# The tail of a fused attention and Fourier kernel: weight rows loaded earlier, the spectrum scaled in 8 and 24 rows, and the transform back along h in two halves

## The chip, the cores and the metric

The kernel runs on one core of a Trainium2 chip. The metric is the time of one execution on the device in microseconds; the median of several executions is compared. Engines are named as in the profile: PE (TensorE; PEld is its weight load), DVE (VectorE), ACT (ScalarE), POOL (GpSimd), SP (SyncE, which here only issues DMAs).

## The reference, cut to what matters

Two layers act on x (4, 64, 96, 96), both as x + f(group_norm(x)). The first is an attention over all 9216 positions of an image (with a sigmoid in place of the softmax), followed by a gate per channel. The second multiplies the lowest 32 by 16 Fourier modes by complex weights, 64 input by 64 output channels for each mode:

```python
u_hat = jnp.fft.rfft2(u, norm='ortho')
top = jnp.einsum('bchw,cohw->bohw', u_hat[:, :, :k_h, :k_w], R_pos)
bot = jnp.einsum('bchw,cohw->bohw', u_hat[:, :, H - k_h:, :k_w], R_neg)
v_hat = jnp.zeros((B, C_out, H, W_half), dtype=u_hat.dtype)
v_hat = v_hat.at[:, :, :k_h, :k_w].set(top)
v_hat = v_hat.at[:, :, H - k_h:, :k_w].set(bot)
return jnp.fft.irfft2(v_hat, s=(H, W), norm='ortho')
```

Everything is float32.

## The kernel before, in words

The four images are handled as two pairs; 128 partitions hold two images' 64 channels. The attention of both pairs is one long stream on PE and ACT (lines 580, 601, 618). The second layer of the first pair is hidden inside the stream of the second. The second layer of the second pair can only begin when the stream has ended: this is the tail, and the change lies there. An image pair is cut into 12 strips of 768 columns (`NSTRIP`, `STRIP`).

The steps of the tail, in order of time:

- Reload of the layer's input. `again` lies in the space of `vT`; the last piece is issued by SP at L880 when the stream ends. Seven strips are combined with it on DVE (L183), five (`ADDED`: 4, 5, 6, 8, 10) are scaled on ACT (L983) and completed by an accumulating DMA that POOL issues (L984).
- Strips. For each, DVE transposes (L991, into `xt`, places `t0` to `t3`), ACT sums squares (L996), and PE transforms along w (L1003). After each third of the strips DVE transposes the result (L1009, places `a0` to `a2`) and PE transforms along h (L1015).
- Spectrum. DVE transposes (L1050, place `s`), then DVE and ACT scale by the group's deviation into `u` (L1055 to L1063), in two halves of 16 of the 32 rows `h`; between them the constant mode is corrected (L215).
- Mixing. For each `q` from 0 to 7 four rows `h` are multiplied by their weight rows (L230), in two halves that are copied out by DVE and by ACT in turn (L125, L127). The results of `q` 0 to 5 go through DRAM (`vd`, issued by SP at L248) and come back in another order as `vt` (L286, issued by ACT and SP); those of `q` 6 and 7 are put in place by a matrix `picks` on PE (L269) and added by DVE (L274).
- Transform back along h. 16 matmuls (L1105), each with 64 rows of input, two of which sit side by side in the array, one for each image; then eight transposes on DVE (L1112).
- Transform back along w: for each strip four matmuls (L1122, two halves of the strip, two halves of the rows), one addition on DVE to the strip of x1 (L1130; strip 0 in two halves) and one output DMA (L1131, SP and ACT in turn). `ps_y` has three buffers.

The 32 weight rows of the mixing arrive from several sides: nine in `early` during the stream, two and four (`w_mid`) in the tail's own space, nine by POOL into the space of `vT` as the strips are done with it (L1072), and the last eight by SP (L941) into the places `a0`, `t0` to `t3`, `a1`, `a2` and `s`, each as soon as its place is free. SP issues its DMAs in the order of the program.

`occupy(n, ...)` sends n matmuls without use to PE behind a given instruction (L964): four before the strips, three after the statistics, one after the `picks`, three after the transform back along h.

The scheduling: inside `with tc.manual_schedule(...)` each engine runs its instructions in the order in which they are written; elsewhere in the tail a list scheduler orders them.

Of the kernel before, what the change touches and what calls it, by code (L numbers as in the profile page):

```python
# [33 lines left out]
F32 = mybir.dt.float32  # L34
F32R = mybir.dt.float32r
AF = mybir.ActivationFunctionType
ALU = mybir.AluOpType
# [3 lines left out]
P = 128  # L41
B, C, H, W = 4, 64, 96, 96
# [4 lines left out]
KW = 16  # L47
KH = 32
NB = 512
# [9 lines left out]
ENGINES = {mybir.EngineType.PE, mybir.EngineType.Activation, mybir.EngineType.DVE}  # L59
LAG = 8  # L60
SIDE = 4
U = KH * KW * 4
UPAD = 4 * SIDE
STRIP = 8 * W
SQ = 32
NSQ = H // SQ
NSTRIP = N // STRIP
# [14 lines left out]
NSLOT = 6  # L82
NLATE = 3 * NSQ * P
NPICK = 2
PICK = P + 4 * (NPICK - 1)
# [3 lines left out]
def tile_kernel(ctx: ExitStack, tc: tile.TileContext, x, cst, late, spec, out):  # L89
    nc = tc.nc  # L90
    xf = x.rearrange("b c h w -> (b c) (h w)")
    outf = out.rearrange("b c h w -> (b c) (h w)")
# [6 lines left out]
    cs = const.tile([P, NCONST], F32, tag="cs", name="cs")  # L99
    xs = []  # L100
    for p in range(NPAIR):
        xt = xpool.tile([P, N], F32, tag=f"x{p}", name=f"x{p}")
        for s in range(9):
            parts = 2 if p == 0 and s == 8 else 1
            for i in range(parts):
                cols = bass.ts(parts * s + i, N // 9 // parts)
# [8 lines left out]
    def named(name, rows=P):  # L115
        return cs[:rows, PLACE[name]]

    pav, nhalf, low_sb, ident = named("pav"), named("nhalf"), named("low"), named("ident")
    turn, moved = [0], [None, None]
# [310 lines left out]
    with tc.tile_pool(name="work", bufs=1) as work, \  # L430
# [6 lines left out]
        banks = ps_s.tile([P, 8, NB], F32, tag="banks", name="banks")  # L437
        spare = [0]

        at = attp.tile([P, 14, NB], F32, tag="at", name="at")  # L440
# [10 lines left out]
        projected = [None]  # L451
# [225 lines left out]
        each, norm0, _ = stats_of(0)  # L677
        with tc.manual_schedule(engines=ENGINES):
# [17 lines left out]
            q, split_queries = first_queries()  # L696
# [25 lines left out]
        early = []  # L722
# [82 lines left out]
        while len(done) < len(sizes):  # L805

            t, was = len(done), done[-1] if done else 0
            n = max(1, -(-was // TILES))
# [76 lines left out]
        with tc.manual_schedule(engines=ENGINES):  # L885
# [5 lines left out]
            for t in range(T):  # L891
# [14 lines left out]
                i, put_by = 0, []  # L906
# [13 lines left out]
        gate, steps, f = after(1)  # L920
# [7 lines left out]
    with tc.tile_pool(name="tail", bufs=1, reuse_waits="tile") as tail, \  # L928
            ExitStack() as banks:

        def psum(name, bufs=1):
            return banks.enter_context(
                tc.tile_pool(name=name, bufs=bufs, space=PSUM, reuse_waits="tile"))
# [18 lines left out]
            wts[NSLOT - 4 + i] = w_mid[:, bass.ts(i, KW * C)]  # L952
            nc.gpsimd.dma_start(wts[NSLOT - 4 + i], spec[NSLOT - 4 + i])

        picks = tail.tile([P, SIDE * PICK], F32, tag="pick", name="picks")
        nc.gpsimd.dma_start(picks, late[:, NLATE:])

        def occupy(n, behind, pool):


            pd = pool.tile([P, NB], F32, tag="idle", bufs=1, name=f"idle_{behind.ins.name}")
            with tc.issue_after(behind.ins):
                for _ in range(n):
                    nc.tensor.matmul(pd, cs[:, :P], cs[:, :NB], start=True, stop=True)  # L964

        small_bank = psum("ps_m")
        l1 = Layer1(1, gate, lambda name: small_bank.tile([P, NB], F32, tag="m", name=name),
                    evacuate, (nc.sync, nc.scalar))
        l1.wts = wts
        occupy(4, projected[0], small_bank)  # L970
        x1 = xs[1]

        mr, steps, mv = group_stats(None, l1.bank, "l1_1")
# [54 lines left out]
        with tc.manual_schedule(engines=ENGINES):  # L1028
            for s in range(NSTRIP):
                if s not in ADDED:  # L1030
                    l1.combine(s, again[:, bass.ts(s, STRIP)])
                strip(s)
                if s in (1, 3):
                    steps[s // 2]()
                if s == 5:
                    rows_turned(0)
                    rows(0)
                if s == 9:
                    rows_turned(1)
            var = small.tile([P, 1], F32, tag="var", name="var")  # L1040
            nc.vector.tensor_reduce(var, squares, AX.X, ALU.add)
            nc.vector.tensor_scalar(mv[:, 1:2], var, 1.0 / N, None, ALU.mult)
            steps[2]()
            steps[3]()
            rows_turned(2)
            rows(1)
            rows(2)
            l1.spread(mr)
            for b in range(2):
                nc.vector.transpose(t[:, bass.ts(b, NB)],  # L1050
                                    pu[b].rearrange("q (c k) -> q k c", k=KW))
            for half in range(2):
                h = bass.ts(half, KH // 2)
                for b in range(2):
                    nc.scalar.activation(u[:, :, :, h, 0, b], tb[b][:, :, :, h], AF.Copy,  # L1055
                                         scale=l1.rs[:, 0, b:b + 1])
                    nc.vector.tensor_scalar(u[lo, :, :, h, 1, b], tb[b][hi, :, :, h],
                                            l1.rs[hi, 1, b:b + 1], None, ALU.mult)
                    if b == 0:
                        nc.vector.tensor_scalar(u[hi, :, :, h, 1, b], tb[b][lo, :, :, h],  # L1060
                                                l1.rs[lo, 0, b:b + 1], None, ALU.mult)
                    else:
                        nc.scalar.activation(u[hi, :, :, h, 1, b], tb[b][lo, :, :, h], AF.Copy,  # L1063
                                             scale=l1.rs[lo, 0, b:b + 1])
                if half == 0:
                    l1.constant_mode()
        occupy(3, l1.last, small_bank)

        for i in range(9):
            h = NSLOT + 9 + i  # L1070
            wts[h] = again[:, bass.ts(i, KW * C)]
            nc.gpsimd.dma_start(wts[h], spec[h])  # L1072
        late_rows = iter(range(NSLOT + 18, KH))
        for tag in ("a0", "t0", "t1", "t2", "t3", "a1", "a2", "s"):
            weight(tag, next(late_rows), nc.sync)

        l1.vms = [tail.tile([P, KW * C], F32, tag="vm", bufs=4, name=f"vm_{q}")
                  for q in range(4)] + early[:4]
        banks.close()
        mix_bank = psum("ps_v", 1)  # L1080
        l1.bank = lambda name: mix_bank.tile([P, NB], F32, tag="v", name=name, bufs=7)
        l1.place_of_vt = lambda: place_of("w0", "vt")
        gh = tail.tile([P, 2 * P], F32, tag="gh", name="gh_in_fours")
        for q in range(KH // 4):
            l1.mix(q, 0)
            if q == 0:
                with tc.issue_after(moved[0].ins):
                    nc.vector.memset(gh, 0.0)
                    for e in range(2):
                        nc.vector.tensor_copy(  # L1090
                            gh[:, bass.ts(e, P)].rearrange("q (j i) -> q j i", j=4)[:, :, :H // 4],
                            named("gh")[:, bass.ts(e, H)].rearrange("q (i j) -> q j i", j=4))
            l1.mix(q, 1)
        l1.pick(picks)
        occupy(1, l1.last, mix_bank)


        banks.close()
        pz_bank, NO = psum("ps_z"), C // 4
        pz = [[pz_bank.tile([P, NB], F32, tag=f"z{b}{i}", name=f"pz_{b}_{i}") for i in range(4)]  # L1100
              for b in range(2)]
        for i in range(4):
            for e in range(2):
                for b in range(2):
                    last = nc.tensor.matmul(  # L1105
                        pz[b][i][:, bass.ts(e, KW * NO)], gh[bass.ts(b, 2 * KH), bass.ts(e, P)],
                        l1.vt[bass.ts(b, 2 * KH), :].rearrange("q (k o) -> q k o", o=C)[
                            :, :, bass.ts(i, NO)], start=True, stop=True)
        z = tail.tile([P, P, SQ], F32, tag="z", name="z_1")
        for i in range(4):  # L1110
            for b in range(2):
                nc.vector.transpose(z[:, b * C + i * NO:b * C + (i + 1) * NO, :],  # L1112
                                    pz[b][i].rearrange("q (k o) -> q o k", o=NO))
        banks.close()
        py_bank = psum("ps_y", 3)
        occupy(3, last, py_bank)
        for s in range(NSTRIP):
            py = py_bank.tile([P, 2, NB], F32, tag="y", name=f"py_{s}")
            for i in range(2):
                for r in range(2):  # L1120
                    rows = bass.ts(r, C)
                    nc.tensor.matmul(py[:, r, bass.ts(i, 2 * W)], z[rows, :, 2 * s + i],  # L1122
                                     named("gw")[rows, bass.ts(r, 2 * W)], start=True, stop=True)
            for i in range(2 if s == 0 else 1):
                n = STRIP // 2 if s == 0 else STRIP
                cols = slice(s * STRIP + i * n, s * STRIP + i * n + n)
                o = x1[:, cols].rearrange("q (i r m) -> q i r m", r=2, m=2 * W)
                from_py = py[:, :, 2 * W * i:2 * W * i + n // 2].rearrange(
                    "q r (i m) -> q i r m", m=2 * W)
                nc.vector.tensor_tensor(o, from_py, o, ALU.add)  # L1130
                (nc.sync, nc.scalar)[(s + i) % 2].dma_start(outf[bass.ts(1, P), cols], x1[:, cols])  # L1131


def _constants(l0):
# [24 lines left out]
    for b in range(2):  # L1159
        rows = slice(b * C, (b + 1) * C)  # L1160
        at = PLACE["wv"].start
        for i, w in enumerate(("wv", "wq", "wk")):
            n = len(l0[w])
# [29 lines left out]
    for n in range(SIDE):  # L1193
        pick = np.zeros((P, PICK))
        for g in range(4):
            for slot in range(2):
                for i in range(2):
                    pick[32 * g + 4 * n + 2 * slot + i, 64 * i + 32 * slot + KH - 4 + g] = 1.0
        b.append(pick)
    return a, np.concatenate(b, 1).astype(np.float32)  # L1200


# [28 lines left out]
```

## Time and profile before

| | us |
|---|---|
| median of 4 runs | 3028.34 (3027.92 to 3029.68) |
| the profiled execution, its own time | 3031.53 |
| its span in the profile | 3029.7 |
| end of the attention stream (last L618) | 2950.0 |
| first matmul of the mixing (L230) | 2982.9 |
| first matmul of the transform back along h (L1105) | 3003.4 |
| first addition of a strip (L1130) | 3012.9 |
| end of the last addition | 3023.6 |

Times inside the profile are counted from the start of the span. In the rows of the chain of waits the columns are start, length and what ran. In rows by group they are line, engine, operation, output<-inputs, shape and count, then busy time, mean duration in ns, and the idle time of the engine ahead of them. In rows by stretch they are the stretch, its length, the busy time of PE, PEld, DVE, ACT and POOL with the number of instructions, the TensorE clock that was granted as a share of the full one, the mean busy share of the 16 DMA engines, and GB/s. A float32 matmul shows as two records.

### The profile page before, as it was taken

The numbers are of one execution on the slowest core, as the hardware profiler recorded it, in microseconds if no ns is written. First come the engines' busy times: TensorE is split into PE (matmuls) and PEld (weight loads), VectorE is DVE, ScalarE is ACT, GpSimd is POOL, SyncE is SP. The second block draws the span as 40 slices with busy tenths as digits, with TensorE's granted clock in tenths as the row PEclk, the third lists the DMA queues.
The fourth block names the chain that finished last, engine by engine and source line by source line (L and its number), as shares of the span: only waits on it lengthen the run. The fifth ranks groups of instructions, "written<-read, shape, count | busy, mean of one in ns | idle before, by whom it ended". The sixth has DMA issues, their size and how long they took to land.

```text
span 3029.7 us, 44108 instructions
## 1 busy us (share of the span) xinstructions
PE 3011.0 (99%) x19364; PEld 1113.2 (37%) x19364; DVE 308.2 (10%) x706; ACT 2416.8 (80%) x1555; POOL 69.9 (2%) x138
## 2 busy tenths in 40 slices
PE   9999999999999999999999999999999999999998
PEld 4333333333333333333433333333333333333336
DVE  6300000000000000002411101100000000000006
ACT  4788888888888888887788887778778888888873
POOL 0100000000000000001300000000001000000001
PEclk9999999999999999999999999999999999999999
DMA  4100000000000000001422322412113000000027
GB/s 159 32 4 4 4 4 4 4 4 4 2 3 4 4 4 4 4 4 32 99 67 69 85 79 86 134 33 45 51 46 125 4 4 4 4 4 4 1 63 249
DMA packets 114609, 117.09 MB, mean 39 GB/s; under 512 B 77488, under 2 KB 84784, under 8 KB 114320
## 3 DMA queue, kind: packets, MB, share of 16 engines
q1 hardware_dynamic: 105536, 92.82, 11.2%
q0 software_dynamic: 7472, 18.56, 2.0%
q8 instruction: 152, 2.49, 0.3%
q10 hardware_dynamic: 1408, 2.88, 0.3%
q14 instruction: 41, 0.34, 0.0%
HBM read 79.94 MB, written 32.31 MB: 37 GB/s over the span
## 4 chain that ended last, share of the span: by engine, by line
PE 98%; DVE 1%; DMA 0%; ACT 0%; issue 0%; POOL 0%; ACTq 0%; DVEq 0%
PE banks L618 77%; PE banks L580 17%; PE banks L499 1%; PE banks L230 1%; PE banks L671 0%; DVE x L1130 0%; PE pv L230 0%; PE banks L421 0%; PE pa L1003 0%; ACT at L601 0%; PE banks L344 0%; PE pz L1105 0%; PE pu L1015 0%; PE banks L464 0%; DVE xt L991 0%
## 5 line engine op out<-in xcount | busy, mean ns | idle before, releaser
L601 ACT ACTIVATE at<-banks 128x2048 f32<-128x2048 f32 (+1 forms) x1501 | 2388.3, 1642 | 533.7 <-PE banks L580 521.8
L618 PE MATMUL banks<-at,vT 128*64 128x512 f32 (+1 forms) x11824 | 2402.2, 547 | 0.0
L618 PEld LDWEIGHTS banks<-at,vT 128*64 128x64 f32 x11824 | 778.1, 136 | 1362.3 <-issue 1307.2
L580 PE MATMUL banks<-q,kT 32*128 32x512 f32 x5040 | 542.7, 452 | 0.8 <-ACT at L601 0.7
L580 PEld LDWEIGHTS banks<-q,kT 32*128 32x128 f32 x5040 | 223.8, 182 | 447.5 <-issue 331.2
L624 DVE SCALAR_TENSOR_TENSOR x<-banks,x 128x512 f32<-128x512 f32 x36 | 24.9, 691 | 2023.1 <-PE banks L618 1945.2
L550 POOL DMA_DIRECT2D stage<-qk x96 | 47.7, 504 | 932.2 <-DMA qk<-turned 928.7
L425 DVE TENSOR_TENSOR x<-banks,x 128x768 f32<-128x768 f32 x12 | 11.5, 958 | 168.5 <-PE banks L421 168.5
L499 PEld LDWEIGHTS banks<-cs,x 64*64 64x64 f32 x1152 | 21.9, 135 | 17.3 <-ACT at L601 13.1
L506 DVE TENSOR_TENSOR vT<-banks,cs 128x256 f32<-128x256 f32 x72 | 26.8, 412 | 0.0
L499 PE MATMUL banks<-cs,x 64*64 64x80 f32 (+1 forms) x1152 | 26.0, 234 | 0.0
L626 DVE TENSOR_REDUCE maxs<-x 128x1 f32<-128x512 f32 x36 | 24.7, 686 | 1.3
L632 DVE BATCH_NORM_STATS2 stats<-x 128x6 f32<-128x512 f32 x36 | 22.5, 682 | 3.9 <-DMA x<-in_x_dram 3.9
L736 DVE COPY ws<-banks 128x512 f32<-128x512 f32 x16 | 11.1, 691 | 115.3 <-PE banks L230 115.3
L163 POOL TENSOR_TENSOR mr_l<-ve_l,cs 128x1 f32<-128x1 f32 x4 | 2.2, 558 | 837.2 <-DVE ve_l L162 837.2
L736 DVE COPY ae<-banks 128x512 f32<-128x512 f32 x6 | 4.1, 691 | 157.3 <-issue 114.9
L984 POOL DMA_DIRECT2D x<-vT x5 | 4.5, 1035 | 659.9 <-ACT x L983 659.9
L671 PE MATMUL banks<-x 128*128 128x256 f32 (+1 forms) x48 | 14.5, 464 | 4.8 <-DMA x<-in_x_dram 4.8
L580 PE MATMUL banks<-q_first,kT 32*128 32x512 f32 x144 | 17.1, 459 | 1.8 <-ACT at L601 1.1
L537 DVE STREAM_TRANSPOSE turned<-t 128x384 f32<-128x384 f32 (+1 forms) x35 | 17.9, 511 | 1.2
L170 DVE TENSOR_SCALAR x<-x,mr_l 128x512 f32<-128x512 f32 x36 | 17.6, 529 | 0.7 <-POOL mr_l L163 0.7
L1003 PE MATMUL pa<-xt,lc 128*128 128x256 f32 x72 | 16.8, 385 | 0.6 <-DVE mr_l L152 0.3
(145 smaller groups left out, 429.1 us busy)
## 6 DMA issues: line engine op xcount, KB each, us to landing
ws<-in_spec_dram SPq DMA_DIRECT2D x20, 512.0 KB
q<-qk SPq DMA_DIRECT2D x280, 32.0 KB
x<-in_x_dram SPq DMA_DIRECT2D x17, 512.0 KB
out_dram<-x SPq DMA_DIRECT2D x17, 384.0 KB
room<-in_spec_dram SPq DMA_DIRECT2D x12, 512.0 KB
old<-in_x_dram SPq DMA_DIRECT2D x12, 384.0 KB
qk<-turned SPq DMA_DIRECT2D x96, 48.0 KB
x1d<-x SPq DMA_DIRECT2D x12, 384.0 KB
```

The costliest lines, as they stand in the source:

```text
L170: nc.vector.tensor_scalar(dst, src, mr[:, 0:1], mr[:, 1:2], ALU.subtract, ALU.mult)
L230: self.last = nc.tensor.matmul(pv[bass.ts(g, 32), :].rearrange("q (n k o) -> q n k o", n=SIDE, o=C)[:, :, k, :], self.ut[:, at:at + 32], s ...
L499: projected[0] = nc.tensor.matmul(pp[bass.ts(e, P // 2), b, 2 * a + h, :width], src[rows, a, h, bass.ts(e, P // 2)], named("wv")[rows, :wi ...
L506: nc.vector.tensor_tensor(vT[:, 4 * s:4 * s + 4, bass.ts(b, C)].rearrange("p (h a) m -> p a h m", h=2), pp[:, b, :, :C].rearrange("p (a h) ...
L537: nc.vector.transpose(turned[:, k:].rearrange("p k a (m h) -> p (k a) h m", h=2), t[:, k:].rearrange("p k a h m -> p (k a) h m").bitcast(F32))
L550: nc.gpsimd.dma_start(come[bass.ts(r, QK), :], split[p][s][:, r % 2, bass.ts(r // 2, NB // 2)])
L580: nc.tensor.matmul(banks[:, bank_of(i), :], kT[r:r + 32, i % TILES // 8, i // 4 % 2, :], ask[i // TILES][r:r + 32, :], start=True, stop=True)
L601: nc.scalar.activation(at[:, of:of + n, :], banks[:, bank:bank + n, :], AF.Sigmoid)
L618: attended[0] = nc.tensor.matmul(acc[half, cols], vT[:, j, half], at[:, place(2 * pair + b), cols], start=(j == 0), stop=(j == NCH - 1 and ...
L624: nc.vector.scalar_tensor_tensor(blk, acc, 1.0, blk, ALU.mult, ALU.add, accum_out=sums[p][:, m:m + 1])
L626: mark[0] = nc.vector.tensor_reduce(maxs[p][:, m:m + 1], blk, AX.X, ALU.max)
L632: each = [lambda s=s: nc.vector.bn_stats(stats[:, s, :], xs[p][:, bass.ts(s, NB)]) for s in range(NBLK)]
```

## The change

- Four of SP's eight weight rows (24 to 27) get places of their own, `r0` to `r3`, and are issued directly behind the picks' load in the program, that is behind L880 on SP; the other four (28 to 31) follow as before into `a0`, `a1`, `a2` and `s`. The four buffers `vm` move into the places `t0` to `t3`.
- The spectrum is scaled in a part of 8 rows and one of 24.
- The matrix of the transform back along h comes from the host, in the same DMA as `picks` (1040 columns, 528 before), and is no longer arranged on DVE. It is block diagonal over the two images: one matmul takes all 128 rows and yields one half of the 96 rows h for both images, with 12 of 16 places filled.
- The transform back along h is done in two halves (`along_h_back`): the first ahead of all strips; the second in four steps whose matmuls stand between those of strips 0 to 4 and whose transposes follow the additions of strips 1 to 4. Strips 0 to 5 need the first half alone. `ps_z` keeps four banks, `ps_y` has two buffers.
- The weights of L1122 are read from `z` at a step of 16 elements, 32 before.
- Matmuls without use: three before the strips (four before), one of 256 columns after the picks (512 before), none after the transform back along h (three before).

```diff
-        picks = tail.tile([P, SIDE * PICK], F32, tag="pick", name="picks")
+        picks = tail.tile([P, SIDE * PICK + 4 * P], F32, tag="pick", name="picks")
         nc.gpsimd.dma_start(picks, late[:, NLATE:])
+        gh = picks[:, SIDE * PICK:].rearrange("q (n e m) -> q n e m", n=2, e=2)
+
+        late_rows = iter(range(NSLOT + 18, KH))
+        for i in range(4):
+            weight(f"r{i}", next(late_rows), nc.sync)
...
-        occupy(4, projected[0], small_bank)
+        occupy(3, projected[0], small_bank)
...
-            for half in range(2):
-                h = bass.ts(half, KH // 2)
+            for h in (slice(0, 8), slice(8, KH)):
...
-                if half == 0:
+                if h.start == 0:
                     l1.constant_mode()
...
-        late_rows = iter(range(NSLOT + 18, KH))
-        for tag in ("a0", "t0", "t1", "t2", "t3", "a1", "a2", "s"):
+        for tag in ("a0", "a1", "a2", "s"):
             weight(tag, next(late_rows), nc.sync)
 
-        l1.vms = [tail.tile([P, KW * C], F32, tag="vm", bufs=4, name=f"vm_{q}")
-                  for q in range(4)] + early[:4]
+        l1.vms = [place_of(f"t{q}", f"vm_{q}") for q in range(4)] + early[:4]
...
-            if q == 0:
-                with tc.issue_after(moved[0].ins):
-                    nc.vector.memset(gh, 0.0)
-                    for e in range(2):
-                        nc.vector.tensor_copy(
...
-        occupy(1, l1.last, mix_bank)
+        occupy(1, l1.last, mix_bank, NB // 2)
...
+        pz_bank, py_bank, NO = psum("ps_z"), psum("ps_y", 2), C // 4
+        z = tail.tile([P, 2, 2, C, KW], F32, tag="z", name="z_1")
+
+        def along_h_back(half, i):
+
+            pz = pz_bank.tile([P, NB], F32, tag=f"z{i}", name=f"pz_{half}_{i}")
             for e in range(2):
...
+                nc.tensor.matmul(
+                    pz[:, bass.ts(e, KW * NO)], gh[:, half, e, :],
+                    l1.vt.rearrange("q (k o) -> q k o", o=C)[:, :, bass.ts(i, NO)],
+                    start=True, stop=True)
+            return lambda: nc.vector.transpose(
+                z[:, half, :, bass.ts(i, NO), :].rearrange("q b o i -> q o b i"),
+                pz.rearrange("q (k o) -> q o k", o=NO))
...
+        with tc.manual_schedule(engines=ENGINES):
+            for turn_back in [along_h_back(0, i) for i in range(4)]:
+                turn_back()
+            later = along_h_back(1, 0)
+            for s in range(NSTRIP):
+                if s == 0:
+                    for add in [along_w_back(0, [i]) for i in range(2)]:
+                        add()
+                else:
+                    along_w_back(s, [0, 1])()
+                if 1 <= s <= 4:
+                    later()
+                    if s < 4:
+                        later = along_h_back(1, s)
```

`along_w_back(s, part)` issues the matmuls of a strip or of half a strip and returns the addition and its output DMA.

## The prediction

> **What bounds the kernel now.** The page's slices show PE at 9 tenths until the last one: 2950 us are the attention, which the change leaves alone. I therefore read the chain of waits from there on:
>
> ```profile
> 2979.98 2.79 PE idle_I-15431_15454 L964 x6
> ...
> 2982.88 10.60 PE pv L230 x192
> ...
> 2994.12 3.97 DMA vd<-w_early
> ...
> 2998.64 3.03 DMA vt<-vd
> ...
> 3002.20 1.09 DVE vt L274 x3
> ...
> 3003.37 5.61 PE pz L1105 x31
> 3008.98 2.77 PE idle_I-15718_15732 L964 x6
> 3011.75 1.15 PE py L1122 x8
> ...
> 3012.93 10.63 DVE x L1130 x13
> ```
>
> Mixing, a round trip of the mixed rows through DRAM, the transform along h (`pz`), three dummy matmuls, the transform along w (`py`), and thirteen additions. Then the costs of the last stage, by group (busy, mean ns):
>
> ```profile
> L1122 PE MATMUL py<-cs,z 64*128 64x192 f32 x96 | 10.9, 383 | 0.0
> L1122 PEld LDWEIGHTS py<-cs,z 64*128 64x128 f32 x96 | 10.6, 309 | 0.8 <-issue 0.8
> L1130 DVE TENSOR_TENSOR x<-py,x 128x768 f32<-128x768 f32 x11 | 9.7, 952 | 0.0
> ```
>
> PE and DVE need the same time per strip: 0.874 us (four pairs of records, starts 0.2185 apart) and 0.87 (starts of the additions). Last, sums over stretches, for the granted clock and the DMA share (the two numbers before the GB/s):
>
> ```profile
> 2953.00:2955.70 2.70, 2.69 (x7) 1.25 (x8) 2.40 (x5) 2.67 (x4) 1.23 (x2) 1.00 0.00 0
> ...
> 2966.00:2985.00 19.00, 18.64 (x116) 11.86 (x116) 14.86 (x26) 9.38 (x20) 3.07 (x7) 1.00 1.02 391
> ...
> 3000.37:3003.78 3.41, 1.45 (x6) 0.63 (x6) 1.42 (x4) 0.00 (x0) 0.00 (x0) 1.00 0.02 4
> 3003.78:3007.19 3.41, 3.41 (x19) 2.90 (x18) 1.73 (x3) 0.00 (x0) 0.00 (x0) 0.50 0.00 0
> ...
> 3017.42:3020.84 3.42, 3.42 (x34) 3.42 (x34) 3.42 (x4) 0.00 (x0) 0.00 (x0) 1.00 1.02 389
> ```
>
> DMA is empty before 2955.7 and full from 2966. PE ran at half clock for 3.41 us, just in `pz`, after a stretch with 1.45 us of matmuls. While the strips leave, DMA is full: 393 KB at 396 GB/s is 0.98 us a strip, more than DVE's 0.87. A queue builds up: by the landing records the first whole strip took 2.37 us from issue, the last 5.05 (3023.59 to 3028.64). The span ends at 3029.7; this execution's own time was 3031.53, the runs' median 3028.34. I work out a difference of spans and apply it to the median.
>
> **Part 1, four rows earlier.** Four SP issues of 0.33 us go from behind `a0` (2967.5) to directly behind the reload of L880 (2950.05), and end at 2951.7; nothing on SP waits behind them until 2967.5, so the issues cost nothing. Their data do: L880 and 2.1 MB at 410 GB/s last from 2951.7 to 2957.8. The accumulating reloads (L984) start moving at 2955.7, so up to 2.0 us of DMA work gets in their way. Landings and first use by DVE: strip 4 2958.5/2961.5, strip 5 2961.1/2962.4, strip 6 2962.9/2964.4, strip 8 2965.1/2967.1, strip 10 2968.3/2971.4. Later by 2.0, only strip 5 is late, by 0.7; DVE's idle 0.1 and 0.2 us after it absorb 0.3. Cost: 0 to 0.4, I take 0.2.
>
> In return 5.1 us of transfers leave the full stretch. Weights weren't awaited (PE has no gap in L230), but the stores to `vd` queued behind them: the last took 3.97 us, a 384 KB transfer on an idle queue 3.23.
>
> **Part 2, spectrum in 8 and 24 rows.** Mixing starts after the second L215 (ends 2982.78; PE at 2982.88), although the chain names the dummy matmuls. Three DVE scalings ahead of it (0.44 us for 256 elements, 0.15 of it fixed by the 1-element rows) fall to 0.30: L215 ends near 2982.35. The three dummies occupy PE until 2982.49 (last start 2982.06 plus 0.43), so the gain stops at 0.4. The second part (24 rows) ends on ACT near 2984.6; PE needs it only after q=0 and 1, at 2986.0. Hidden.
>
> Both together: the last store is issued 0.4 earlier and lands up to 0.7 faster. But ACT issues four gathers (0.44 each) and a copy before the last two, so the last gather moves from 2998.64 to about 2998.1: 0.54 (bounds 0 and 1.05). With the 0.2: **-0.34**; `pz` starts at 3003.03. The fewer dummies ahead of strip 0 gain nothing (strip 1 waits for DVE anyway); the removed `gh` preparation (1.1 us of DVE) lay in a 1.0 us gap between copies. Also at nothing: the larger `picks` load (POOL had been idle for 660 us before L984, so it was issued and landed long before), `vm` in the places of `xt` (PE last reads those at 2975.9, the first copy comes at 2984.1), and the rows of `a1`, `a2` and `s`, which SP issues where it did, with less ahead of them; q=7 needs them near 2995.
>
> **Part 3, first half of h.** Now K=128 against a half-empty block matrix: 16 records of 0.2133 that can't share the array, where 32 paired ones took the same 3.41 us. Half the result costs what all of it cost; only four transposes instead of eight follow, and no dummies. With the same half-clock window: 3.5 records until 3003.78, 8 until 3007.19, 4.5 more until 3008.15; 0.2 of latency, the fourth transpose (0.68) ends at 3009.04. Two pairs of `py` need 0.44, latency and semaphores 0.27, and a restart, because the weights are `z` and can't be loaded ahead: 0 to 0.15 (the first pair after a wait took 0.37 instead of 0.22), I take 0.08. First addition 3009.83, 6.80 after `pz` starts instead of 9.56: **-2.76**.
>
> **Part 4, the strips.** DVE gets four transposes (0.60) between additions: 13 additions alone 10.63, with them 13.0. PE has more: in strips 1 to 4 `py` 0.874 plus `pz` 0.853 is 1.73 against DVE's 1.47. And `ps_y` has two buffers instead of three: strip s+2 starts when the addition of s ends. From addition to addition two strips later: 0.95 + 0.06 + 0.08 + 0.874 + 0.22 = 2.18 to 2.24 us, against 1.74. First to second whole strip 1.78, three strips of 1.73, then 1.47 and 1.30 to strip 6, then pairs of 0.87 and 1.30, the last addition 0.95: 15.9 us instead of 10.63: **+5.27**. Bounds 13.0 and 16.3.
>
> **Part 5, the way out.** Strips now come 1.1 to 1.7 apart, DMA needs 0.98: no queue. After the last addition 0.03 + 2.37 + 0.1 + 1.03 (landing to end, as before) = 3.5 instead of 6.1: **-2.6**.
>
> Sum: -0.34 - 2.76 + 5.27 - 2.6 = -0.43 us, so 3027.9. A measurement of this kernel can tell about 0.2%, 6.1 us, from no change; the forecast is no change.
>
> **A rule against the rows.** Loading 128 contiguous columns took 190 ns (L269), the strided ones of `z` 308, and pairs of `py` start 0.2185 apart where their matmuls need 0.16; I keep 0.2185, though the stride halves from 128 to 64 bytes. The Trainium skill ("TensorE: Matmul & The Clock Gate", LDWEIGHTS) gives columns/1.2 ns, 107 here, whatever their place; by it the load would hide and the sum would be -1.9. Its page "SBUF — State Buffer" (the note on cachelines) has 16-byte lines and a price for each new one, which both strides pay, as I assume. The TensorE page's section on psum-queue depth-cycling speaks against the change: small PE pauses while cycling through banks let the clock fall again; no row here shows that in `py`.
>
> **Rivals.**
> *The strips go faster.* If half the stride loads faster, pairs fall towards 0.165, strips 1 to 4 to 1.51 and the two-buffer turn to 2.0: 1.5 less; without the restart 0.4 less. 3026.0. For: the load is what paces `py`. Against: both strides skip.
> *The front pays, or one clock window falls into the strips.* A stall of 0.4 and nothing from the stores: +0.7; one window of 3.41 us at half clock in strips 1 to 4, where a strip would take 2.99 (`py` 4 x 0.32, `pz` 4 x 0.427): up to +2.5. 3030.4.
> *The clock stays at half.* Slower: every 3.41 us window from 3007 on holds waits for one of two `ps_y` buffers and is judged idle. `pz` +1.0, first `py` +0.2, strips 1 to 4 2.99 each, later ones 1.28 (PE-bound): additions 21.7 instead of 15.9. +6.5 on the old span: 3034.9. It decides where PE's share of a window falls to what was punished before: 1.45 of 3.41 us was, 2.08 of 3.00 (2950 to 2953) wasn't; the last six strips would have 1.75 of 2.2, and at half clock PE would be busy throughout and so recover. That speaks against it.
>
> **How the numbers follow.** Forecast 0.62, faster strips 0.22, front or one window 0.10, stuck clock 0.04, unseen gains 0.02. All but the last two lie within 6.1 us of 3028.3: a first addition without any half clock gains 1.7 more, everything favourable together comes to -4.7. Unseen terms of either sign get some more: faster 0.05, same 0.89, slower 0.06. Range: below, 1.9 for faster strips, 0.7 for the front, 0.9 for half of a window that misses `pz`: 3024.4. Above, 2.5 for a window in the strips: 3030.4.
>
> **What would show it.** After the change: L230 starts 0.4 earlier; `vd` lands within 3.5 us; one DVE wait for DMA at strip 5; first addition about 3 us earlier, last one some 2 us later; additions in the last six strips in steps of 0.87 and 1.3 with DVE waiting for `py`; DMA share under 0.9 in the strips. Wrong would be: additions without gaps (PE faster than read), a PE clock of 0.5 after 3010, a `pv` gap for weights, or a transpose into the strided `z` that takes over 0.7.

## The result and the profile after

The changed kernel takes 3032.89 us (median of 42 runs, 3030.81 to 3034.7), the kernel before 3029.11 beside it (60 runs, 3027.5 to 3031.35): the ratio is 1.0013, 95% interval 1.0009 to 1.0017. That is 3.8 us slower (2.7 to 5.1), where 0.4 faster was forecast and 3030.4 was the end of the range. By the prediction's own measure (0.2%) it still is "no change"; by this many runs it is a small loss whose interval does not hold 1. Of the 2.5 us above the range's end 0.8 is the kernel before, which the prediction took at 3028.34.

The profiled execution of the changed kernel has a span of 3030.1 us and took 3031.90. The one of before had met half clock once more at its start (27.36 to 30.77), so its tail began 1.8 us later. The stretches that answer to those shown of before are therefore taken 1.77 earlier (except the last, one clock window in the strips):

```profile
2951.23:2953.93 2.70, 2.68 (x7) 1.25 (x8) 2.40 (x5) 2.67 (x4) 1.23 (x2) 1.00 1.02 417
2964.23:2983.23 19.00, 18.72 (x117) 11.60 (x117) 14.83 (x25) 9.62 (x20) 3.41 (x8) 1.00 0.93 348
2998.58:3001.99 3.41, 1.33 (x7) 0.88 (x6) 1.42 (x4) 0.00 (x0) 0.00 (x0) 1.00 0.01 2
3001.99:3005.40 3.41, 3.41 (x10) 2.70 (x9) 1.43 (x2) 0.00 (x0) 0.00 (x0) 0.50 0.00 0
3015.64:3019.06 3.42, 2.52 (x22) 2.31 (x24) 2.80 (x4) 0.00 (x0) 0.00 (x0) 1.00 0.48 190
```

As forecast the rows fill the empty stretch (DMA share 1.02 instead of 0.00), the full one is relieved (0.93 instead of 1.02), `pz` meets half clock as before, and DMA idles half the time while strips 4 and 5 are made. The chain of waits of the tail:

```profile
2978.21 2.79 PE idle_I-15438_15461 L969 x6
2981.00 0.04 issue
2981.04 10.61 PE pv L230 x192
...
2992.29 3.80 DMA vd<-w_early
...
2996.65 2.88 DMA vt<-vd
...
3000.05 1.08 DVE vt L274 x3
...
3001.22 6.24 PE pz L1100 x20
3007.47 0.72 PE py L1115 x4
...
3008.22 0.57 DVE x L1125
...
3008.83 1.19 PE py L1115 x8
3010.02 1.06 PE pz L1100 x4
3011.08 1.12 PE py L1115 x8
3012.20 1.06 PE pz L1100 x4
3013.26 1.12 PE py L1115 x8
3014.39 1.06 PE pz L1100 x4
...
3016.62 0.96 DVE x L1125
3017.58 0.63 DVE z L1104
...
3018.35 1.20 PE py L1115 x8
...
3024.08 1.84 DVE x L1125 x2
```

In strips 1 to 4 the chain runs over PE alone, `py` and `pz` in turn, and the two pieces add up to 2.18 us, not to the 0.874 + 0.853 = 1.73 of the prediction. By group, DVE, which had no gap behind its first addition in before, now waits 4.9 us for `py`, while a single `py` record hardly takes longer (404 ns, 383 before):

```profile
L1115 PE MATMUL py<-cs,z 64*128 64x192 f32 x96 | 13.0, 404 | 1.5 <-DVE z L1104 0.9 <-DVE x L1125 0.6
L1125 DVE TENSOR_TENSOR x<-py,x 128x768 f32<-128x768 f32 (+1 forms) x13 | 11.3, 892 | 4.9 <-PE py L1115 4.9
L1115 PEld LDWEIGHTS py<-cs,z 64*128 64x128 f32 x96 | 11.1, 304 | 3.8 <-DVE x L1125 1.3 <-PE py L1115 1.1 <-issue 1.0
```

By stages, from the first L160 of the tail (`pv_l`, a small matmul of the statistics; L230 follows 7.1 us later) to the end of the span. The last two columns are kernels e9 and e10 below: the same two kernels with PE's gap ahead of `pz` filled, without half clock in the tail and without the instruction packet that the experiments found.

| us | before | after | e9 (before) | e10 (after) |
|---|---|---|---|---|
| first L160 to first `pz` | 27.64 | 27.26 | 27.68 | 27.64 |
| first `pz` to first addition | 9.55 | 6.99 | 7.69 | 5.31 |
| first addition to end of the last | 10.63 | 17.71 | 10.63 | 17.70 |
| end of the last addition to end | 6.12 | 4.13 | 4.59 | 3.49 |
| sum | 53.94 | 56.09 | 50.59 | 54.14 |

The profiled pair differs by 2.15, the equal pair by 3.55. The first was kind to the change: by 0.3 in the stretch up to `pz`, 0.2 ahead of the first addition, and 0.9 in the way out, which in that execution of the kernel before cost much.

### The profile page after: what moved, and what is told of

It is laid out like the page before. It is cut to its first block, busy times and chain, and to the rows that moved or that the text cites. A ratio compares the mean times of both kernels' runs of the same rounds, so it can differ in the third digit from the quotient of the medians.

```text
span 3030.1 us, 44088 instructions
## 1 busy us (share of the span) xinstructions
PE 3011.2 (99%) x19356; PEld 1111.3 (37%) x19356; DVE 308.3 (10%) x703; ACT 2417.5 (80%) x1555; POOL 69.6 (2%) x138
## 4 chain that ended last, share of the span: by engine, by line
PE 98%; DVE 1%; DMA 1%; ACT 0%; issue 0%; SPq 0%; POOL 0%; ACTq 0%; DVEq 0%
PE banks L618 77%; PE banks L580 17%; PE banks L499 1%; PE banks L230 1%; PE pv L230 0%; PE banks L421 0%; PE pz L1100 0%; DMA x<-in_x_dram 0%; PE py L1115 0%; PE pa L1008 0%; ACT at L601 0%; PE banks L344 0%; DVE xt L996 0%; PE pu L1020 0%; DVE x L1125 0%
```

## The experiments

Each kernel ran 11 times beside the kernel before on the same chip (e7 and e8 five times, e11 and e12 once), and has one profile. "Step" is the distance of two additions. The first theory was: PE is held up at every change between 64-row matmuls (`py`) and 128-row matmuls (`pz`). Its rivals: two buffers for `py`, the clock, the strided weights.

**e1, the front alone.** The kernel before with the four early rows and the 8 and 24 rows.

```diff
+        for i in range(4):
+            weight(f"r{i}", next(late_rows), nc.sync)
-            for half in range(2):
+            for h in (slice(0, 8), slice(8, KH)):
```

> The kernel before with the two front parts of the change alone: four weight rows issued behind L880, the spectrum in 8 and 24 rows (vm in the places t0 to t3); back end, dummies and gh as before. Theory (the loss lies between the strips alone): from the issue of L880 to the first vt addition (L274) 51.4 us as after the change, 51.8 before; time 0.4 below before. Rival (the early rows cost something that one profile does not show): time above before by 1 or more.

3029.65 against 3029.11 (1.0005, 0.9995 to 1.0014): no gain, no loss that can be told. L230 starts 38.49 us after the last reload at L875 is issued, 38.56 in before: 0.07 earlier, not 0.4. The second L215 did end 0.25 earlier against L230's start, but the dummies ahead of it hold PE. By the semaphores the first load of L230 waits for L215 and also for the last dummy to be done. That is told 0.61 us after the dummy's start (2982.06 to 2982.67 in e1), although dummies start 0.43 apart, and L230 follows 0.04 later, as in the chain of the changed kernel above. In before the two signals came almost together, the dummy's at 2982.77 and L215's at 2982.79, so an earlier L215 had next to nothing to gain.

**e2, the whole second half ahead of the strips.** The additions then have only the transposes between them.

```diff
-            later = along_h_back(1, 0)
+            laters = [along_h_back(1, i) for i in range(4)]
...
-                    later()
-                    if s < 4:
-                        later = along_h_back(1, s)
+                    laters[s - 1]()
```

> After, with the second half's eight matmuls (pz) all ahead of the strips; its transposes stay between the additions. Theory A (PE pays about 0.2 us at each change between 128-row and 64-row matmuls, two changes per strip): first addition 2.6 us later than after, then steps of 1.47 (DVE) instead of 2.18 in strips 1 to 4, no change of shape left inside the strips; all additions 15.5 instead of 17.7; time within 0.7 of after. Rival B (two ps_y buffers make the 2.18): steps stay at 2.18, additions 17.7, time 2.5 above after.

3033.28 (1.0016, 1.0007 to 1.0025). Steps of 1.46 to 1.51, DVE without a gap:

```profile
3012.88 0.96 DVE x L1125
3013.83 0.62 DVE z L1104
3014.46 0.84 DVE x L1125
```

So DVE is not what makes 2.18; PE is. This execution also met half clock once in the strips (3019.52 to 3022.93): the rival of one clock window does occur, and here it cost 0.7 us: steps of 1.74 and 1.28 where e12, without it, has 1.45 and 0.87.

**e3, three buffers for `py`, two banks for `pz`.**

```diff
-        ... psum("ps_y", 2)
+        ... psum("ps_y", 3)
-            pz = pz_bank.tile([P, NB], F32, tag=f"z{i}", ...)
+            pz = pz_bank.tile([P, NB], F32, tag=f"z{i % 2}", ...)
```

> After, with ps_z in two banks instead of four and ps_y with three buffers instead of two. Theory A: strips 1 to 4 stay at 2.18 a step, strips 6 to 11 come at 0.88 instead of 1.13; additions 16.3 instead of 17.7, of which the output queue (0.98 a strip) takes back about a third; time 1 below after. Rival B: strips 1 to 4 fall to 1.73 as well, additions 14.5, time 2.5 below after.

3033.29 (1.0011, 1.0002 to 1.0020). Strips 1 to 4 stay at 2.19, 6 to 11 come 0.87 apart: the buffers are not the 2.18. The additions take 16.14 instead of 17.71, yet the kernel gains nothing: the way out is 5.65 instead of 4.13. What had been saved waited for the stores, which led to e7.

**e4, six dummies of 512 columns ahead of `pz`.**

```diff
-        occupy(1, l1.last, mix_bank, NB // 2)
+        occupy(6, l1.last, mix_bank)
```

> After, with six dummy matmuls of 512 columns behind the picks instead of one of 256, so that PE does not rest before pz. Theory C (part of the loss in the median is half clock in the now unpaired pz): no 0.5 in the granted clock between the picks and the last addition, pz in 3.5 instead of 5.9 us, time 1.5 to 2 below after. Rival (the clock is not set by this rest): 0.5 comes as before, time as after.

3032.96 (1.0012, 1.0003 to 1.0021). No half clock, but the six last until `pz` starts, 2.5 us after the changed kernel's; that ate the gain. Steps stay 2.18: it is not the clock either.

**e5 and e6, three such dummies, in the kernel before and in the changed one.** They end before `pz` can start.

```diff
-        occupy(1, l1.last, mix_bank)             # e6: occupy(1, l1.last, mix_bank, NB // 2)
+        occupy(3, l1.last, mix_bank)
```

> The kernel before with three 512-column dummy matmuls in place of one between picking and the transform along h, so that PE has no 2 us gap there (the profile of before has 1.45 us of matmuls in the 3.41 us window that was followed by half clock in pz; of four profiles with such a gap three show that half clock, one, with 1.62 us in the window, doesn't). Theory 'clock share': the half clock costs 1.7 us where it falls, in about half of the executions, so the median falls by 0.5 to 1.7, to 3027.4 to 3028.6, with no half clock in the record between 2950 and 3020. Rival 'the run-to-run spread has another cause': the half clock goes from the record and the median stays within 0.4 of 3029.1.

> The changed kernel with the same three 512-column dummies in that place (its single one has 256 columns), which end before pz can start. Kernel e4 had six, which held pz back by 2.5 us. Theory 'the tail is 2.2 us longer, the rest of the median's 3.8 us is half clock that the changed kernel meets more often': this kernel is 2.0 to 2.5 us behind e5, near 3030.2, and 2.5 or more ahead of the changed kernel's median of 3032.9. Rival 'more than 2.2 is lost at full clock too': it stays 3 or more behind e5, above 3031.0.

3027.94 (0.9997, 0.9988 to 1.0006) and 3032.79 (1.0012, 1.0004 to 1.0021). The first addition comes 1.69 sooner after `pz` starts, in both; the half clock cost both the same. Yet e6 gained nothing over the changed kernel, and it ends 3.6 behind e5, counted from L160 (4.85 in the medians). The rival was right: my theory that everything above 2.2 was half clock fell. What e6 had instead was a way out of 4.97 us: its last strip took 3.90 from issue to landing, although the last strips came 1.13 apart on average and a store needs 0.98, so that no queue should form.

**e7 and e8, the packet of PE's program moved.** In every trace so far the landings of the strips jump once. In before (issue, last landing, by the DMA records): 3016.58, 3019.29; 3017.43, 3022.14; 3018.32, 3023.07; then 0.93 apart to the end. A strip lands in 16 pieces, and 15 of them are on time: those of the strip issued at 3017.43 are down by 3020.21, the last one at 3022.14. The jump coincides with this (by queue, 3010 us to the end, kernel before; packets, MB, share of 16 engines):

```profile
q10 hardware_dynamic: 1008, 2.56, 31.4%
q1 hardware_dynamic: 864, 2.16, 26.8%
q8 instruction: 1, 0.02, 0.4%
```

One packet of 16 KB, 1.39 us long, starting at 3018.95. Queue 8 carries such a packet for every 250 or so of PE's instructions, always at the same place in its program, so I take it for PE's own code; e7 to e10 move it by adding matmuls. In these eight traces the strip that lands late has lost one DMA engine for 1.5 to 2.6 us, and every later strip queues there.

```diff
                     warm(s)
+                if s < 15:
+                    for _ in range(3):
+                        nc.tensor.matmul(banks[:8, 7, :8], xs[0][:, s * NB:s * NB + 8],
+                                         xs[0][:, s * NB:s * NB + 8], start=True, stop=True)
```

> The changed kernel with 45 tiny matmuls (8 columns) among the warm-up matmuls at the start, while x is still being loaded: they shift every later place in PE's program by about 180 instructions. In all six profiles one 16 KB instruction packet of the queue that follows PE's program moves among the last stores (3021.64 in the changed kernel, 3018.95 before), always after some 38,840 PE records, and from then on one strip's last landing comes 1.5 to 2.6 us late and the following ones 0.93 apart. Theory 'fetch': the last packet moves to before 3012, the last strip lands 2.3 to 2.5 us after its issue instead of 3.06, and the kernel gains 0.5 to 0.8 (near 3032.2). Rival 'plain queue': the strips come at 1.1 us on average and the landings keep their delay, wherever the packet is; no gain.

> The kernel before with the same 45 tiny matmuls at the start. Theory 'fetch': without the packet among the last stores the additions, 0.875 apart, run ahead of stores that take 0.93 each by only 0.5 us in all, so the last strip lands 2.6 to 3.2 us after its issue instead of 5.05; the kernel gains 1.2 to 2.2, to 3026.9 to 3027.9. Rival 'plain queue', which is how the prediction read the 5.05: transfers of 0.98 us behind additions of 0.87 build the queue by themselves; the last strip still takes 4.5 or more, and the time stays within 0.5 of 3029.1.

As times a failure: 3044.92 and 3041.24. The tiny matmuls kept PE's clock at half until 27.0 and 28.9 us, which was 8.5 in the changed kernel, and the start took some 12 us longer. As a test of the landings they answer: the packet moved to 3014 and 3018, ahead of the stores, no landing jumps, and the last strip took 2.42 us (e7) and 3.53 (e8).

**e9 and e10, the same tiny matmuls in PE's gap ahead of `pz`.** 80 records in 2.15 us. They end late enough to hold `pz` by 0.3 us in e9 and 0.15 in e10, counted from the last addition to `vt`.

```diff
+                for _ in range(tiny):
+                    nc.tensor.matmul(pd[:8, :8], cs[:, :8], cs[:, :8], start=True, stop=True)
-        occupy(1, l1.last, mix_bank)             # e10: occupy(1, l1.last, mix_bank, NB // 2)
+        occupy(1, l1.last, mix_bank, tiny=40)
```

> The kernel before with 40 tiny matmuls (8 columns, 80 records; in e7 such records started 0.025 us apart at half clock) in PE's 2 us gap ahead of pz: the instruction packet should then move in or before pz, some 220 PE records before the end instead of 62, and pz should start where it did. Theory 'fetch': the last strip lands 3.3 to 3.6 us after its issue, as in e8, and the median falls by 1.2 to 1.8, to 3027.3 to 3027.9. Rival 'the packet only costs where the profile happened to catch it': the landings shorten and the median stays within 0.5.

> The changed kernel with the same 40 tiny matmuls in the same place (behind one dummy of 512 columns instead of 256). Theory 'fetch': the last strip lands 2.4 us after its issue, as in e7 (3.06 in the changed kernel, 3.90 in e6), the median falls by 0.6 to 1.5, to 3031.4 to 3032.3, and the spread of its runs (3030.8 to 3034.7) narrows; the distance to e9 is 3.3 or more at equal clock. Rival 'half clock in the strips makes the rest of the median': the landings shorten, the median stays above 3032.5.

3027.66 (0.9994, 0.9985 to 1.0003) and 3031.11 (1.0005, 0.9996 to 1.0014). The packet is gone from the strips; in e10 it comes at 3008.21, just ahead of the first store (e9, by queue, 3010 to the end):

```profile
q10 hardware_dynamic: 1008, 2.56, 31.3%
q1 hardware_dynamic: 864, 2.16, 26.8%
```

The last strip lands 3.52 after issue in e9, 2.41 in e10. Neither trace has half clock in `pz`, so the medians may hold both effects; the packet alone is read from the landings: 1.5 us in before's profile, 0.64 in the changed kernel's and 1.5 in e6's. It differs from trace to trace (1.1 in e1 and e5): in the changed structure the strips come 1.1 apart on average and some of the delay is caught up. In e11 and e12 below the packet falls among the strips too and delays one by 1.1 and 1.3 us, but the last strip lands 2.42 after its issue, as without it. The two medians differ by 3.45, the traces by 3.55: this is the change at equal clock and without the packet. The runs of e10 also lie closer together (2.5 us instead of 3.9), but these are 11 runs against 42, and the 11 of e2, which has the packet, span 2.0: no narrowing is shown.

**e11 and e12, the change of shape by itself.** e2 with dummies ahead of `py` in strips 1 to 4: two of 128 rows, or four of 64 rows, which fill the same slots.

```diff
+            if 1 <= s <= 4:
+                for r in range(2):               # e12: range(4), rows = bass.ts(r % 2, C)
+                    nc.tensor.matmul(py[:, r, 3 * P:], cs[:, :P], cs[:, :P],
+                                     start=True, stop=True)
```

> Kernel e2 (all of pz ahead, strips 1 to 4 in steps of 1.46) with two dummy matmuls of 128 rows x 128 columns (four records) ahead of py in each of strips 1 to 4, written to columns of py that nothing reads. PE then has 0.87 of py and 0.76 to 0.87 of dummies a strip. Theory 'change of shape costs': each change between 128-row and 64-row matmuls costs 0.2 more, so the steps are 2.0 to 2.2 and the starts at the change lie 0.3 apart instead of 0.22. Rival 'the 2.18 of the changed kernel comes from pz itself (its transposes, its banks, its weights)': steps of 1.6 to 1.8.

> The same as e11 with four dummies of 64 rows in pairs instead of two of 128 rows: the same four slots on PE, but the shape of py throughout. Theory 'change of shape costs': steps of 1.65 to 1.8, 0.35 to 0.45 shorter than in e11, although it has twice the instructions. Rival 'pz itself', or 'every extra block on PE costs': the same steps as in e11.

The chain of e11 stays on PE:

```profile
3011.82 1.12 PE py L1119 x8
3012.94 0.64 PE py L1114 x4
3013.58 1.12 PE py L1119 x8
```

and that of e12 on DVE:

```profile
3014.62 0.96 DVE x L1130
3015.58 0.62 DVE z L1104
3016.20 0.84 DVE x L1130
```

Steps of 1.76 against 1.46 (the times, one run each, 3032.84 and 3033.56, are too few to compare). Both are shorter than I had expected, since dummies with side-by-side weights start 0.11 apart, not 0.2. The distance is the point: in e12 PE needs 1.364 us a strip (record starts 3013.490, 3014.851, 3016.215), in e11 1.765 for the same slots. The starts show where, counted from the last record ahead: into the dummies 0.309 instead of 0.210, behind their first record 0.213 instead of 0.102, back into `py` 0.205 instead of 0.105, behind its first pair 0.365 instead of 0.260. Four times 0.10, two at each change: 0.40 a strip.

**e13 and e15, the back end of before with more taken away; e15 with the front of the change.** Tiny matmuls as in e9, two dummies instead of three behind `pz`, and `z` stored so that the weights of `py` lie side by side.

```diff
-        z = tail.tile([P, P, SQ], F32, tag="z", name="z_1")
+        z = tail.tile([P, SQ, P], F32, tag="z", name="z_1")
-        occupy(3, last, py_bank)
+        occupy(2, last, py_bank)
```

> The back end of the kernel before with three edits: the 40 tiny matmuls in PE's gap (e9, -1.7), two dummies instead of three between pz and py (in e9 py starts 0.37 after the last transposition's end; 0.15 to 0.2 of it is the dummies), and z stored so that the 128 weights of one py matmul lie side by side (pairs of py start 0.212 apart; in e12 matmuls with side-by-side weights of 128 columns started 0.105 apart, so the pace should fall to the 0.16 of 192 columns). The first whole strip's addition then comes 0.17 + 8 x 0.05 = 0.6 earlier, and everything behind it is paced by the stores. Theory 'stores pace the end from the first strip on': 0.4 to 0.7 below e9's 3027.7, so 3027.0 to 3027.3. Rival 'transposing to places 512 bytes apart costs DVE more than the weights gain': at e9's time or above it.

> e13 and the front of the change (four rows early, spectrum in 8 and 24 rows, as in e1). The prediction gave the front -0.34. Theory 'the front is worth 0.1 or less': in nine traces the first addition to vt comes 57.3 to 57.7 us after the first stream reload without it and 57.2 to 57.6 with it, so the median is within 0.3 of e13. Rival 'the front is worth what was forecast': 0.3 to 0.5 below e13. The best of the kernels if so.

3028.11 (0.9997, 0.9988 to 1.0006) and 3029.38 (1.0002, 0.9993 to 1.0011): no better than e9. The intervals of the three overlap, but the traces tell them apart: the first addition comes 9.29 us after `pz` in e13 and e15, 7.69 in e9. The rival was right, in e13's groups:

```profile
L1114 DVE STREAM_TRANSPOSE z<-pz 128x512 f32<-128x512 f32 x8 | 7.1, 1012 | 1.3 <-PE pz L1107 1.3
```

1.01 us each instead of 0.69, eight in a row, against a pace of `py` that did fall (from one pair to the next 0.155 us pass instead of 0.212, 0.162 instead of 0.218 from start to start). And the front brought nothing again.

**e14, the changed kernel with `z` stored so.**

```diff
-        z = tail.tile([P, 2, 2, C, KW], F32, tag="z", name="z_1")
+        z = tail.tile([P, 2, KW, 2, C], F32, tag="z", name="z_1")
```

> The changed kernel with z stored so that the weights of py lie side by side instead of 64 bytes apart. Theory 'the strided weights pace py, and the change of shape is a cost of its own': pairs of py 0.16 apart instead of 0.212, strips 1 to 4 in steps of 1.93 to 2.0 instead of 2.18 (py 0.64, pz 0.85, two changes 0.44), additions 16.0 to 16.8 instead of 17.7, median down by 0.5 to 1.3. Rival 'the strided load is the whole of the 0.44': steps of 1.5 to 1.6. Rival 'py is paced by something else': steps stay at 2.18.

3032.11 (1.0010, 1.0001 to 1.0019). From one pair of `py` to the next 0.155 to 0.159 us pass, and steps fall to 1.91. The step alone does not decide, because DVE now needs as much (0.95 + 0.97 on the chain); the starts do: at the two changes of a strip 0.252 and 0.320, 0.309 and 0.260, where steady records have 0.157 and 0.216: 0.39 us, with weights that are not strided. With strided ones it was 0.44 (0.307, 0.320, 0.309, 0.371): the stride's share is 0.05. The additions take 16.11 us instead of 17.71; in this profile the packet cost the way out 1.6 again (5.12 us).

**e16, the changed structure with all this together**: e10, `z` as in e14, three buffers as in e3.

```diff
-        ... psum("ps_y", 2)
+        ... psum("ps_y", 3)
-        z = tail.tile([P, 2, 2, C, KW], F32, tag="z", name="z_1")
+        z = tail.tile([P, 2, KW, 2, C], F32, tag="z", name="z_1")
+        occupy(1, l1.last, mix_bank, tiny=40)
```

> What the changed structure reaches with every cost met so far taken away but the change of shape: e10's tiny matmuls, z as in e14, three buffers for py as in e3. Theory 'change of shape and DVE's 1.47 a strip remain': first addition as in e10 (5.3 after pz starts), steps 1.93 to 2.0 in strips 1 to 4 and 0.87 to 0.95 later, additions 14.7 to 15.5; the stores take 0.93 each, so the way out is 3.9 to 4.4: 3029.2 to 3030.2, behind e13 by 2 or more. Rival 'the two halves pay once PE is relieved': below 3028.

3029.54 (1.0003, 0.9995 to 1.0012). First addition 6.2 after `pz`, since four transposes at 1.0 come first, additions 15.23, way out 4.02. It draws level with the kernel before and stays 1.4 to 1.9 behind e13 and e9.

**e17 and e18, e9 with two dummies behind `pz`, and e9 again.**

```diff
-        occupy(3, last, py_bank)
+        occupy(2, last, py_bank)
```

> Kernel e9 with two dummies instead of three between pz and py, z as in the kernel before (e13 showed that transposing to places 512 bytes apart costs DVE 1.0 us each instead of 0.67). In e9 py starts 0.37 after the last transposition's end, of which 0.15 to 0.2 are the dummies. Expected: first addition 0.1 to 0.25 earlier after pz's start than e9's 7.69, median 0 to 0.3 below e9 run beside it. Rival 'a gap ahead of py brings half clock': above e9.

> Kernel e9 once more on another chip's runs, since its interval against the kernel before (0.9985 to 1.0003) just holds 1. Expected as in e9: 1.0 to 2.0 us below the runs beside it, last strip landing 3.4 to 3.6 us after its issue. Rival 'e9 was luck': within 0.5.

3027.72 (0.9995, 0.9986 to 1.0005) and 3027.75 (0.9997, 0.9988 to 1.0005). In e17 the first addition comes 7.37 after `pz` instead of 7.69. The 22 runs of e9 and e18 have a median of 3027.7, the 42 runs of the kernel before beside them 3028.9. About 1 us better than the kernel before, then, but each interval for itself still holds no change. The last strip of e18 lands 3.55 after its issue, as expected; its median is only 0.5 below the runs beside it, where 1.0 to 2.0 was expected and 1.7 had come out in e9. So the landings repeat, and what they are worth in the median is not settled.

## Why the prediction was wrong, step by step

The forecast was -0.43; the equal pair gives +3.55 and the medians +3.8, whose interval (2.7 to 5.1) holds the pair's value too.

- **Parts 1 and 2, the front** (forecast -0.34; equal pair from L160 to `pz` -0.04, e1 no gain). The stall of DVE was small, as said (0.1), with the reloads landing 0.8 to 2.1 later. Two steps failed. One is "the gain stops at 0.4": the last dummy starts at 2982.16, not at 2982.06 as was read, and L230 waits until its end is told, 0.61 after its start, where 0.43 was put; that left 0.07. The other is "lands up to 0.7 faster": the last store to `vd` took 3.80 to 4.28 us in the thirteen traces with the front and 3.83 to 4.35 in the seven without. From L160 to the end of the last addition to `vt` it is 27.40 on average with the front and 27.49 without, where equal kernels differ by 0.4.
- **Part 3** (-2.76; measured -2.56 and -2.38). Right in mechanism, 0.2 to 0.4 short. Of the 0.2 in the profile 0.07 is the restart of `py` (0.155, not 0.08), and 0.1 lies in `pz`: its first record takes 0.29 and the steady ones 0.216 where 0.2133 was put for each. The further 0.2 of the equal pair was not followed.
- **Part 4, the strips** (+5.27, bounds +2.4 and +5.7; measured +7.08). This is the largest miss. The plan (PE-bound, then DVE, then two-buffer turns) held but for strip 6: 1.50, 1.45, then 0.87 and 1.38 for the forecast 1.47, 1.30, 0.87 and 1.30. The size of one PE strip did not: 2.185 instead of 1.73, three times, 1.37 us. The two numbers added were both right, each in a steady run of its own kind; their alternation was nowhere in the sum, and by e11 and e12 it is what costs the 0.4 a strip. It was in the trace: in before, from `pa` (128 rows) to `pu` (64 rows) 0.309 us pass where 0.216 is usual, and the first pair after it takes 0.526 for 0.43. I had even seen 0.37 for 0.22 at the first `py` and called it a wait. Of the remaining 0.4, 0.15 is strip 6: the prediction let it wait for a buffer, but in the chain it waits for the last transposition of the second half (L1104), and its step is 1.45 with two buffers and with three (e3). Another 0.15 lies at the two later turns of the buffers.
- **Part 5, the way out** (-2.6; equal pair -1.10, profiles -1.99). 3.5 was right for the changed kernel without the packet (3.49). The failed step is the reading of before's 6.1 as "a queue builds up": the plain queue makes 4.59, and 1.5 is PE's code on one DMA engine, which the changed kernel meets as well. It is 1.1 in e1 and e5, so before's profile was an expensive one.
- **The rule against the rows.** The Trainium skill ("TensorE: Matmul & The Clock Gate", LDWEIGHTS) gives 107 ns for 128 columns and says nothing of how they lie. For weights side by side e12 and e14 fit it: from start to start 0.112 us with 128 moving columns and 0.162 with 192, which is what the matmuls need by themselves (512 columns take 0.43), so that the load is hidden. For strided ones the rows hold (0.218, at 64 as at 128 bytes). The 190 ns that I had set against the rule is the duration of one load's record, not its pace.
- **What the 0.10 might be.** It is about the length of one such load left uncovered: 0.320 behind a change is 0.213 and 0.107. The Trainium skill ("TensorE: Matmul & The Clock Gate", Packing small matmuls) says that a load overlaps running matmuls only where their row groups differ, though it also names a background buffer for weights. Steady runs show overlap without different row groups: the 128-row records of `pz` start 0.216 apart, which their 256 columns need by themselves, so their loads are covered. Only behind a change does it fit. No run here shows the cause.
- **The rivals.** "The strips go faster" did not occur; half the stride changed nothing. "The clock stays at half" did not occur: 1.00 from 3005.4 until the strips were done. One window in the strips was seen once (e2). None of them had the mechanism that decided.

Adding the misses: 0.3 for the front, 0.4 for Part 3, 1.8 for the strips, 1.5 for the way out make 4.0, from -0.43 to +3.55. How often half clock falls into the strips of the changed kernel, and what that adds to the spread of its runs, was not settled.

## What to carry to other kernels

Add up steady paces only within one shape of matmul: look in the trace for the first two records behind each change, and count them for every change that an interleaving creates. Before a drain at the end is put down to a queue, compare the first and the last piece of each transfer, and look for a packet of another queue on the one engine that is late. Count a matmul that something waits for until its end is told, not until the next one can start. Profiles of two executions can differ by more than the change: compare them stage by stage, and at the same granted clock.

## What was not expected of the hardware

- A change between matmuls of 64 and of 128 rows cost PE 0.10 us at the first record and 0.10 at the one after it (float32, 128 to 256 columns); with strided weights 0.15 at the second.
- The end of a 512-column matmul was told 0.61 us after its start (before, e1, changed kernel), where such matmuls start 0.43 apart.
- One 16 KB packet of PE's program (0.9 to 1.8 us) among the stores delayed the late pieces of a strip by 1.1 to 2.6 us, and until that was caught up the stores were paced by that one engine at 0.93 us per 384 KB.
- DVE transposed 128x512 into single places 512 bytes apart in 1.01 to 1.03 us on average, into runs of 16 elements in 0.71 and into runs of 32 in 0.68 to 0.69.
- Matmuls of 8 columns started 0.025 us apart, and when they were mixed with 256-column ones at the start PE's clock stayed at half until 27.0 and 28.9 us (e7, e8; 7.4 to 10.3 in the other traces).
